# Own issue tables for the first and the last graph of a two-layer graph network on one Trainium2 core

## The chip, the cores and the metric

The kernel runs on one core of one Trainium2 chip. A core has five engines that each work through their own queue in order: TensorE (PE, matrix products; PEld is its loading of weights), VectorE (DVE), ScalarE (ACT), GpSimd (POOL) and SyncE (SP), which here issues all the DMA transfers. Times are device microseconds for one execution. The median of three runs of the kernel before is 1805.68 us (1802.11 to 1806.99); the execution that the profile shows took 1803.61 us, of which 1801.8 us are its span from the first to the last instruction.

## What is computed

There are 16 graphs of 1024 nodes with 256 features, and an adjacency matrix of 1024 x 1024 integers for each. The matrix is symmetric, holds zeros and ones, and has ones on the diagonal. Two layers follow each other; each ends in a residual sum and a normalization of rows.

```python
def _L0_gnn_ref(hidden, adj, a0, a1, a2, a3, bias):
    e_of = lambda a: _leaky(jnp.einsum('bid,bjd->bij', h * a[:, 0], h))
    alpha = jnp.where(adj == 1, e0, neg_inf)      # kinds 2, 3, 4 likewise
    alpha = jax.nn.sigmoid(alpha)
    return jnp.einsum('bij,bjd->bid', alpha, h) + bias

def _L1_gnn_ref(X, A, W, a_src, a_dst):
    Wh = (X @ W).reshape(B, N, H, F)              # 4 heads of 64
    e = leaky_relu(e_src[:, :, None, :] + e_dst[:, None, :, :], 0.2)
    alpha = softmax(where(A > 0, e, -1e9), axis=2)
    Hout = elu(einsum('bijh,bjhf->bihf', alpha, Wh))

x = _layernorm(x + _L0_gnn_ref(x, adj, ...))
x = _layernorm(x + _L1_gnn_ref(x, adj, ...))
```

## The kernel before, in words

The nodes of a graph are cut into eight blocks of 128. A graph's work is cut into stages, each a Python generator whose every step issues a few instructions. The table `TIMES` gives a due time in us for each step of each stage, relative to the graph's own start; graph b's steps are moved by 112 x b (`PERIOD`). `issue` (L861) sorts all steps of all 16 graphs by due time and runs them in that order. So the table fixes only the order in which instructions stand in each engine's queue, never a moment: an instruction runs as soon as it is at the head of its queue and its inputs are there. Due times of neighbouring graphs interleave, so that graph b+1's first layer is made while graph b is in its second.

The first layer of a graph, in the order of the data:

- `xload` (L231) fetches the nodes xb in one transfer of 1 MB; `aload` (L236) fetches the adjacency in eight row blocks of 512 KB into two buffers (a32).
- `cast` (L244, ACT) makes a block bf16 (a16, one buffer) and adds it up; `turn` (L253) transposes it by a DMA from the SP queue (aT, one buffer); `mask` (L259, ACT) squares it into the byte mask mT and adds that up.
- `xt` (L271, PE) transposes the nodes, `xtc` (L281, ACT) copies them out of PSUM, and `xta` (L291, ACT) multiplies them by the factors a0.
- `score` (L306, PE) makes the upper triangle of scores in twelve pieces; `leak` (L319, ACT), `leaky` (L327, DVE) and `sigmoid` (L333, ACT) turn each into a gate; `upper` (L363, DVE) masks a row of it, and `below` (L344, PE) with `lower` (L352, DVE) fills the lower triangle from the transposed upper one.
- `agg` (L370, PE) sums the nodes by the gates, 16 products for each pair of row blocks; `residual`, `moments`, `gathered`, `spread`, `shift` and `norm` (L388 to L439) are the residual and the normalization.

The second layer: `yt`, `ytc`, `project` and `wh` (L442 to L479) make the heads. `top_dve` (L506) ends with nd, the negated target terms. `exps` (L545) makes exponential factors es. For each of four heads and two slopes, `product` (L556, DVE) multiplies the 64 columns of a head by its factors (prod), `high` (L571, ACT) rounds the product and `low` (L577, DVE) takes what is left; both go into gm. `sload` (L585) fetches the source terms of a head, spread over all partitions (sbc); prod and sbc share four buffers. `pos` (L595, DVE) makes a 0/1 matrix (six buffers), `acc` (L605, PE) multiplies gm by it, `acc_low` (L620, ACT) and `acc_sum` (L629, DVE) collect it into u. `all_edges` (allm) and `total` do the same for the whole mask. `weigh` (L688, DVE) multiplies a part of u by rho, `divide` (L699, DVE) adds the parts and multiplies by the reciprocal of the softmax sum; `elu` (L729, ACT), `join` (L717, DVE), a second normalization and `leave` end the graph. After the last graph a small check (L1032 to L1050) decides whether a general path has to run; with these inputs it doesn't.

All PSUM tiles of one bank (nodes, scores, gates, sums) come from one pool of four buffers, `ps_t`.

Of the kernel before, what the change touches and what calls it, by code (L numbers as in the profile page):

```python
# [10 lines left out]
BF16 = mybir.dt.bfloat16  # L11
# [3 lines left out]
AF = mybir.ActivationFunctionType  # L15
ALU = mybir.AluOpType
# [11 lines left out]
P = 128  # L28
# [8 lines left out]
def load_constants(nc, const, work, x, a_list, bias, w, a_src, a_dst):  # L37
    k = Consts()
    B, N, D = x.shape
    H, F = a_src.shape  # L40
    k.B, k.N, k.D, k.H, k.F = B, N, D, H, F
    k.NB, k.DC, k.NH, k.WA = N // P, D // P, N // HALF, D + H
    k.WD = k.WA + H
    k.F1 = F + 2
    k.ident = const.tile([P, P], F32, name="ident")
    make_identity(nc, k.ident)
    k.mhalf = const.tile([P, 1], F32, name="mhalf")
    nc.gpsimd.memset(k.mhalf, -0.5)

    k.a_sb = const.tile([P, k.DC, NK], F32, name="a_sb")  # L50
    for i, a in enumerate(a_list):
        nc.sync.dma_start(out=k.a_sb[:, :, i : i + 1], in_=a.rearrange("(c p) o -> p c o", p=P))
    bias_bc = work.tile([P, D], F32, tag="bias_bc", name="bias_bc")
    nc.sync.dma_start(out=bias_bc, in_=bias.partition_broadcast(P))


    k.w_aug = const.tile([P, k.DC, k.WD], F32, name="w_aug")
    nc.sync.dma_start(out=k.w_aug[:, :, 0:D], in_=w.rearrange("(c p) f -> p c f", p=P))
    for a, which in ((a_src, 0), (a_dst, 1)):
        a_bc = work.tile([P, D], F32, tag="a_bc", name=f"a_bc{which}")  # L60
        nc.sync.dma_start(out=a_bc, in_=a.rearrange("h f -> (h f)").partition_broadcast(P))
        for c in range(k.DC):
            prod = work.tile([P, D], F32, tag="prod", name=f"prod{which}_{c}")
            nc.vector.tensor_tensor(prod, k.w_aug[:, c, 0:D], a_bc, ALU.mult)
            dst = k.w_aug[:, c, D + which * H : D + which * H + H]
            nc.vector.tensor_reduce(dst, prod.rearrange("p (h f) -> p h f", h=H), AX.X, ALU.add)

    k.ones_r = const.tile([P, P], F32R, name="ones_r")
    ones = work.tile([P, P], F32, tag="ones", name="ones")
    nc.gpsimd.memset(ones, 1.0)  # L70
    nc.scalar.copy(k.ones_r, ones)
    k.ones = k.ones_r.bitcast(F32)
    b_hi = work.tile([P, D], F32R, tag="b_hi", name="b_hi")
    nc.scalar.copy(b_hi, bias_bc)
    b_lo = work.tile([P, D], F32, tag="b_lo", name="b_lo")
    nc.vector.tensor_tensor(b_lo, bias_bc, b_hi.bitcast(F32), ALU.subtract)
    nc.vector.tensor_scalar(b_lo, b_lo, k.ident[:, 1:2], None, ALU.mult)
    k.bias_r = const.tile([P, D], F32R, name="bias_r")
    nc.vector.scalar_tensor_tensor(
        k.bias_r, b_hi.bitcast(F32), k.ident[:, 0:1], b_lo, ALU.mult, ALU.add  # L80
    )
    return k
# [127 lines left out]
def stages(nc, k, pl, b, xg, adjg, outg, gm, sums, span, zinv):  # L210


    H, F, D, N, NB, DC, NH = k.H, k.F, k.D, k.N, k.NB, k.DC, k.NH
    F1, WD = k.F1, k.WD
    NQ = NB // NH
    HEADS = [(half, h) for half in range(NH) for h in range(H)]

    TOTALS = [*range(NQ, NB), *range(NQ)]
    t = {}

    def bank(name):
# [30 lines left out]

    def turn():  # L253
        for ib in range(NB):
            t["aT", ib] = pl.adjp.tile([P, NB, P], BF16, tag="aT", name="aT", bufs=1)
            nc.sync.dma_start_transpose(out=t["aT", ib], in_=t["a16", ib])
            yield

    def mask():  # L259
# [21 lines left out]
    def xtc():  # L281
        t["xT"] = pl.big.tile([P, DC, N], F32, tag="xT", name="xT")
        for c in range(DC):
            for half in range(NH):
                nc.scalar.copy(
                    t["xT"][:, c, half * HALF : (half + 1) * HALF],
                    t["xt", c, half].rearrange("p q n -> p (q n)"),
                )
                yield

    def xta():  # L291
        for jb in range(NB):
            xTa = t["xTa", jb] = pl.work.tile([P, DC, P], F32, tag="xTa", name="xTa", bufs=2)
            for c in range(DC):
                nc.scalar.activation(  # L295
                    xTa[:, c, :], t["xT"][:, c, jb * P : (jb + 1) * P], AF.Copy,
                    scale=k.a_sb[:, c, 0:1],
                )
            yield


# [254 lines left out]
    def product():  # L556
        for h, s in FACTORS:
            prod = t["prod", h, s] = pl.work.tile(
                [P, NB, F], F32, tag="sbc", name="prod", bufs=4
            )  # L560
            nc.vector.tensor_tensor(  # L561
                prod, t["wh"][:, :, h * F : (h + 1) * F],
                t["es"][:, s, :, h : h + 1].to_broadcast([P, NB, F]), ALU.mult,
            )
            yield

    def factor(h, s):
# [117 lines left out]

    PAIRS = [(half, pair) for half in range(NH) for pair in range(NQ // 2)]

    def weigh():  # L688
        for half, pair in PAIRS:
            ib = half * NQ + 2 * pair  # L690
            u2 = parts(half, pair)[:, :, :, 1, :]
            if half:
                nc.vector.tensor_tensor(u2, t["ts", pair], u2, ALU.subtract)
                yield
            rho = t["rho"][:, ib : ib + 2].unsqueeze(3)
            nc.vector.tensor_tensor(u2, u2, rho.to_broadcast([P, 2, H, F1]), ALU.mult)
            yield

    def divide():  # L699
        t["rz"] = small("rzs", NB, H)  # L700
        for half, pair in PAIRS:
            ib = half * NQ + 2 * pair
            u = parts(half, pair)
            u1 = u[:, :, :, 0, :]
            nc.vector.tensor_tensor(u1, u1, u[:, :, :, 1, :], ALU.add)
            yield
            rz = t["rz"][:, ib : ib + 2]
            nc.vector.tensor_scalar(rz, u[:, :, :, 0, F], Z_MIN, None, ALU.max)
            yield
            nc.vector.reciprocal(rz, rz)  # L710
            yield
            o = u[:, :, :, 0, 0:F]
            nc.vector.tensor_tensor(o, o, rz.unsqueeze(3).to_broadcast([P, 2, H, F]), ALU.mult)
            yield


# [18 lines left out]
    def leave():  # L735
# [10 lines left out]
        xload=xload(), aload=aload(), cast=cast(), turn=turn(), mask=mask(),  # L746
        xt=xt(), xtc=xtc(), xta=xta(), score=score(), leak=leak(), leaky=leaky(),
        sigmoid=sigmoid(), below=below(), lower=lower(), upper=upper(), agg=agg(),
        residual=residual(), moments0=moments("0"), gathered0=gathered("0"),
        spread0=spread("0"), shift0=shift("0"), norm0=norm("0"),  # L750
        yt=yt(), ytc=ytc(), project=project(), wh=wh(), sources=sources(), rows=rows(), keep_rows=keep_rows(),
        top_dve=top_dve(), top_pe=top_pe(), exps=exps(),
        product=product(), high=high(), low=low(),
        sload=sload(), pos=pos(), acc=acc(), acc_low=acc_low(), acc_sum=acc_sum(),
        all_edges=all_edges(), total=total(), total_kept=total_kept(), total_less=total_less(),
        weigh=weigh(), divide=divide(), elu=elu(), join=join(),
        moments1=moments("1"), gathered1=gathered("1"),
        spread1=spread("1"), shift1=shift("1"), norm1=norm("1"), leave=leave(),
    )

# [93 lines left out]
    "norm1": [242.99, 243.17, 243.83, 247.18, 275.70, 276.83, 276.86, 278.99],  # L856
    "leave": [252.45, 280.64],
}


def issue(graphs):  # L861

    steps = []
    for b, stages in enumerate(graphs):
        for name, times in TIMES.items():
            steps += [(b * PERIOD + at, stages[name]) for at in times]
    for _, stage in sorted(steps, key=lambda step: step[0]):
        next(stage)
# [121 lines left out]
def gnn_resnorm_kernel(  # L990
# [64 lines left out]
    with tc.If(general > 0):  # L1055
        with ExitStack() as slow:
            pl = Pools(slow, tc, "g")
            k.w_dst_rep = pl.big.tile([P, k.DC, H, P], F32, tag="w_dst_rep", name="w_dst_rep")
            replicate(nc, k, k.w_dst_rep, D + H)
            k.ident16 = pl.big.tile([P, P], BF16, tag="ident16", name="ident16")  # L1060
            make_identity(nc, k.ident16)
            k.bias_bc = pl.big.tile([P, D], F32, tag="bias_bc", name="bias_bc")
            nc.sync.dma_start(out=k.bias_bc, in_=bias.partition_broadcast(P))
            with tc.For_i(0, k.B) as b:
                xg = x[bass.ds(b, 1)].rearrange("o n d -> (o n) d")
                adjg = adj[bass.ds(b, 1)].rearrange("o n m -> (o n) m")
                outg = out[bass.ds(b, 1)].rearrange("o n d -> (o n) d")
                xb, a16, y = load_graph(nc, k, pl, xg, adjg)
                alphaT = gate_any_kind(nc, k, pl, xb, a16)
                finish_graph(nc, k, pl, xb, a16, y, alphaT, outg)  # L1070
# [32 lines left out]
```

## Time and profile before

| what | us |
|---|---|
| median of three runs | 1805.68 |
| profiled execution | 1803.61 |
| its span | 1801.8 |
| PE busy | 1721.5 (96%) |
| VectorE busy | 1626.5 (90%) |
| ScalarE busy | 1181.7 (66%) |
| GpSimd busy | 111.4 (6%) |
| first product of `score` | 35.55 |
| first product of `agg` | 61.88 |
| median from issue to landing: adjacency block | 4.9 |
| the same: DMA transpose | 3.1 |
| the same: sbc | 4.5 |

In a line of the profile, L248 is the line of the kernel, out<-in are the tiles, 128x1024 is partitions x elements, and an arrow in brackets names what ended the idle time before the instruction. A group's line gives the number of instructions, their busy time, the mean ns of one, and the idle time before them. The mean of one holds also the time in which the next one already begins, so instructions that follow each other start closer than that.

### The profile page before, as it was taken

What the parts mean: (1) busy time and instruction counts of PE and PEld (TensorE: products, weight loads), DVE (VectorE), ACT (ScalarE), POOL (GpSimd) and SP (SyncE); (2) the same over time, 40 slices, a digit from 0 to 9 for tenths busy, and PEclk for the clock granted to TensorE, in tenths of its full rate; (3) what the DMA queues carried; (4) which work ended last, traced back from release to release, by engine and by line L of the source; (5) the groups of instructions that cost most, each with busy time, mean ns of one, the idle gap of its engine ahead of it and who ended that gap; (6) DMA issues with size and microseconds to landing.
All of it is one profiled execution on the core that took longest, in us unless ns stands there. A gap on an engine that the chain in (4) does not pass through costs nothing.

```text
span 1801.8 us, 29518 instructions
## 1 busy us (share of the span) xinstructions
PE 1721.5 (96%) x10643; PEld 1515.6 (84%) x10643; DVE 1626.5 (90%) x3577; ACT 1181.7 (66%) x2671; POOL 111.4 (6%) x136
## 2 busy tenths in 40 slices
PE   2999999999999999999999999999999999999983
PEld 1769899897988989799898989989898998979873
DVE  1467999999999999999999999999999999999997
ACT  4583775958568495766849476694957759484442
POOL 0000001000010100001010000100000010000100
PEclk8999999999999999999999999999999999999997
DMA  5523352433335243343433344243333424321111
GB/s 155 140 74 85 82 142 65 112 107 79 109 89 139 73 106 96 86 120 88 118 94 99 90 89 129 73 128 100 80 91 105 130 65 122 108 66 42 24 48 43
DMA packets 257689, 170.69 MB, mean 95 GB/s; under 512 B 141696, under 2 KB 241152, under 8 KB 257536
## 3 DMA queue, kind: packets, MB, share of 16 engines
q1 hardware_dynamic: 257536, 168.73, 35.3%
q8 instruction: 86, 1.41, 0.3%
q14 instruction: 67, 0.55, 0.1%
HBM read 118.10 MB, written 17.04 MB: 75 GB/s over the span
## 4 chain that ended last, share of the span: by engine, by line
PE 90%; DVE 3%; issue 3%; ACT 2%; DMA 1%; POOL 0%; SPq 0%; ACTq 0%; POOLq 0%; DVEq 0%
PE acc L611 26%; PE agg L377 25%; PE tot L654 14%; PE e L310 13%; PE pw L466 6%; PE pg L349 3%; PE pt L447 1%; PE pt L276 1%; DVE pos L599 1%; PE agg L373 1%; DMA a<-in_adj_dram 1%; DMA aT<-a 1%; DVE gm L581 0%; ACT a L248 0%; DVE prod L561 0%
## 5 line engine op out<-in xcount | busy, mean ns | idle before, releaser
L599 DVE SCALAR_TENSOR_TENSOR pos<-sbc,nd,mT 128x512 fp32r<-128x512 f32 x1024 | 730.3, 741 | 41.3 <-PE acc L611 40.5
L611 PE MATMUL acc<-gm,pos 128*128 128x264 f32 x4096 | 626.9, 298 | 17.2 <-DVE u L634 11.9
L611 PEld LDWEIGHTS acc<-gm,pos 128*128 128x128 f32 x4096 | 545.1, 190 | 41.7 <-issue 13.0
L377 PE MATMUL agg<-xb,gate 128*128 128x256 f32 x2048 | 474.5, 380 | 1.8 <-DVE gate L366 1.8
L377 PEld LDWEIGHTS agg<-xb,gate 128*128 128x128 f32 x2048 | 375.5, 190 | 46.3 <-DVE gate L366 2.0
L654 PE MATMUL tot<-gm,allm 128*128 128x264 f32 x2048 | 322.5, 299 | 2.7 <-ACT allm L646 1.7
L626 ACT COPY low<-acc 128x264 f32<-128x264 f32 x256 | 89.7, 376 | 314.8 <-PE acc L611 310.0
L654 PEld LDWEIGHTS tot<-gm,allm 128*128 128x128 f32 x2048 | 281.5, 189 | 7.6 <-ACT allm L646 2.2
L310 PE MATMUL e<-xT,xTa 128*128 128x512 f32 (+3 forms) x768 | 272.7, 493 | 10.5 <-ACT xTa L295 10.0
L310 PEld LDWEIGHTS e<-xT,xTa 128*128 128x128 f32 x768 | 133.5, 192 | 103.9 <-issue 47.3
L646 ACT CAST allm<-mT 128x512 fp32r<-128x512 uint8 x256 | 156.8, 619 | 27.5 <-PE tot L654 27.5
L434 ACT ACTIVATE y<-y,shift,rstd 128x256 f32<-128x256 f32 x256 | 137.5, 592 | 47.4 <-DVE shift L427 47.4
L263 ACT ACTIVATE mT<-aT 128x1024 uint8<-128x1024 bf16 x128 | 135.4, 1058 | 27.6 <-DMA aT<-a 27.6
L248 ACT ACTIVATE a<-a 128x1024 bf16<-128x1024 int32 x128 | 135.3, 1057 | 10.5 <-DMA aT<-a 6.4
L330 DVE TENSOR_TENSOR gate<-e,gate 128x512 f32<-128x512 f32 x192 | 104.1, 549 | 39.2 <-ACT gate L322 39.1
L417 POOL TENSOR_SCALAR std<-mv 128x4 f32<-128x4 f32 x64 | 30.1, 470 | 1676.0 <-DVE mv L400 1523.3
L466 PE MATMUL pw<-w_aug,yT 128*128 128x264 f32 x512 | 124.2, 386 | 0.2 <-ACT yT L456 0.2
L634 DVE TENSOR_TENSOR u<-acc,low 128x264 f32<-128x264 f32 x256 | 104.1, 417 | 6.5 <-ACT low L626 6.5
L466 PEld LDWEIGHTS pw<-w_aug,yT 128*128 128x128 f32 x512 | 92.7, 190 | 13.2 <-ACT yT L456 0.7
L394 DVE BATCH_NORM_STATS2 st<-y 128x6 f32<-128x256 f32 x256 | 101.9, 414 | 0.6
L322 ACT ACTIVATE gate<-e 128x512 f32<-128x512 f32 x192 | 93.1, 485 | 11.8 <-PE e L310 11.8
L366 DVE TENSOR_TENSOR gate<-gate,mT 128x1024 f32<-128x1024 f32 (+7 forms) x128 | 94.6, 750 | 4.7 <-PE pg L349 2.9
(92 smaller groups left out, 1771.8 us busy)
## 6 DMA issues: line engine op xcount, KB each, us to landing
a<-in_adj_dram SPq DMA_DIRECT2D x128, 512.0 KB, 4.9
sbc<-sdram SPq DMA_DIRECT2D x128, 256.0 KB, 4.5
xb<-in_x_dram SPq DMA_DIRECT2D x16, 1024.0 KB, 5.8
out_dram<-y SPq DMA_DIRECT2D x32, 512.0 KB, 3.5
aT<-a SPq DMA_TRANSPOSE x128, 3.1
sdram<-srow SPq DMA_DIRECT2D x32, 8.0 KB, 1.4
w_aug<-in_L_gnn_W_dram SPq DMA_DIRECT2D x1, 256.0 KB, 4.6
bias_bc<-in_L_gnn_bias_dram SPq DMA_DIRECT2D x1, 128.0 KB, 4.2
```

Source lines behind the costliest of these rows:

```text
L248: nc.scalar.activation(t["a16", ib], t["a32", ib], AF.Copy, accum_out=sums[:, 0, at : at + 1])
L263: nc.scalar.activation(t["mT"][:, :, ib * P : (ib + 1) * P], t["aT", ib], AF.Square, accum_out=sums[:, 1, at : at + 1],)
L310: nc.tensor.matmul(e[:, 0:n], lhsT=t["xTa", jb][:, c, :], rhs=t["xT"][:, c, at : at + n], start=(c == 0), stop=(c == DC - 1),)
L330: nc.vector.tensor_tensor(ge, t["e", jb, at][:, 0:n], ge, ALU.max)
L377: nc.tensor.matmul(agg[:, 0:D], lhsT=t["gate"][:, jb, ib * P : (ib + 1) * P], rhs=t["xb"][:, jb, :], start=False, stop=(jb == NB - 1),)
L434: nc.scalar.activation(y, y, AF.Identity, bias=t["shift" + which, half][:, q : q + 1], scale=t["rstd" + which, half][:, q : q + 1],)
L466: nc.tensor.matmul(pw[:, 0:WD], lhsT=t["yT"][:, c, jb * P : (jb + 1) * P], rhs=k.w_aug[:, c, :], start=(c == 0), stop=(c == DC - 1),)
L599: nc.vector.scalar_tensor_tensor(p_, t["sbc", half, h], t["nd"][:, jb, h : h + 1], t["mT"][:, jb, half * HALF : (half + 1) * HALF], ALU.is ...
L611: nc.tensor.matmul(t["acc", half, h, q // 2][:, q % 2, 0 : 4 * F1], lhsT=t["pos", half, h, jb][:, q * P : (q + 1) * P], rhs=gm[:, h, jb].r ...
L634: nc.vector.tensor_tensor(t["u", half, pair][:, :, h, :], t["acc", half, h, pair][:, :, 0 : 2 * F1], t["low", half, h, pair], ALU.add,)
L646: nc.scalar.copy(m_, t["mT"][:, j0 : j0 + 4, ib * P : (ib + 1) * P])
L654: nc.tensor.matmul(tot[:, 0 : H * F1], lhsT=t["allm", ib, jb // 4 * 4][:, jb % 4, :], rhs=gm[:, :, jb, l, 1, :], start=(jb == 0 and l == 0 ...
```

## The change

There are two more tables of the same form, `FIRST` for graph 0 and `LAST` for graph 15; graphs 1 to 14 keep `TIMES`. In `FIRST` all steps of graph 0's first layer up to the statistics lie ahead of every step of graph 1, where in `TIMES` graph 1's loads, casts, transposes and masks are mixed in. In `LAST` most of graph 15's second layer lies after the end of graph 14.

In graph 0, moreover, `turn` transposes on PE into PSUM (with a bf16 identity that is now made at the start), eight 128x128 pieces a block, and `xtc` and `xta` run on DVE. In graph 15, the multiplies of `product`, `weigh` and `divide` run on ACT, in pieces that have one factor per partition: eight for a product, eight for a pair of row blocks.

```diff
+    k.ident16 = const.tile([P, P], BF16, name="ident16")
+    make_identity(nc, k.ident16)
...
+    first, last = b == 0, b == k.B - 1
...
     def turn():
         for ib in range(NB):
-            t["aT", ib] = pl.adjp.tile([P, NB, P], BF16, tag="aT", name="aT", bufs=1)
-            nc.sync.dma_start_transpose(out=t["aT", ib], in_=t["a16", ib])
+            if first:
+                t["aT", ib] = pl.ps_t.tile([P, NB, P], BF16, tag="pt", name="pa")
+                for jb in range(NB):
+                    nc.tensor.transpose(
+                        t["aT", ib][:, jb, :], t["a16", ib][:, jb * P : (jb + 1) * P], k.ident16
+                    )
+            else:
+                t["aT", ib] = pl.adjp.tile([P, NB, P], BF16, tag="aT", name="aT", bufs=1)
+                nc.sync.dma_start_transpose(out=t["aT", ib], in_=t["a16", ib])
             yield
...
-                nc.scalar.copy(
+                copy = nc.vector.tensor_copy if first else nc.scalar.copy
+                copy(
                     t["xT"][:, c, half * HALF : (half + 1) * HALF],
...
-                nc.scalar.activation(
-                    xTa[:, c, :], t["xT"][:, c, jb * P : (jb + 1) * P], AF.Copy,
-                    scale=k.a_sb[:, c, 0:1],
-                )
+                part, a = t["xT"][:, c, jb * P : (jb + 1) * P], k.a_sb[:, c, 0:1]
+                if first:
+                    nc.vector.tensor_scalar(xTa[:, c, :], part, a, None, ALU.mult)
+                else:
+                    nc.scalar.activation(xTa[:, c, :], part, AF.Copy, scale=a)
...
-            nc.vector.tensor_tensor(
-                prod, t["wh"][:, :, h * F : (h + 1) * F],
-                t["es"][:, s, :, h : h + 1].to_broadcast([P, NB, F]), ALU.mult,
-            )
+            if last:
+                for jb in range(NB):
+                    nc.scalar.activation(
+                        prod[:, jb, :], t["wh"][:, jb, h * F : (h + 1) * F], AF.Copy,
+                        scale=t["es"][:, s, jb, h : h + 1],
+                    )
+            else:
+                nc.vector.tensor_tensor(
+                    prod, t["wh"][:, :, h * F : (h + 1) * F],
+                    t["es"][:, s, :, h : h + 1].to_broadcast([P, NB, F]), ALU.mult,
+                )
...
+    def times(val, by):
+        if last:
+            for q in range(2):
+                for h in range(H):
+                    nc.scalar.activation(
+                        val[:, q, h, :], val[:, q, h, :], AF.Copy, scale=by[:, q, h : h + 1]
+                    )
+        else:
+            by = by.unsqueeze(3).to_broadcast(list(val.shape))
+            nc.vector.tensor_tensor(val, val, by, ALU.mult)
...
-            rho = t["rho"][:, ib : ib + 2].unsqueeze(3)
-            nc.vector.tensor_tensor(u2, u2, rho.to_broadcast([P, 2, H, F1]), ALU.mult)
+            times(u2, t["rho"][:, ib : ib + 2])
...
-            o = u[:, :, :, 0, 0:F]
-            nc.vector.tensor_tensor(o, o, rz.unsqueeze(3).to_broadcast([P, 2, H, F]), ALU.mult)
+            times(u[:, :, :, 0, 0:F], rz)
...
+FIRST = {
+    "xload": [-2609.24],
+    "aload": [-1820.92, -1748.01, -1728.96, -1693.97, -1643.68, -1598.12, -1550.35, -1517.97],
...
+LAST = {
+    "xload": [-104.45],
...
+    "product": [93.84, 98.53, 107.41, 108.99, 117.90, 120.96, 121.69, 130.00],
...
     for b, stages in enumerate(graphs):
-        for name, times in TIMES.items():
+        table = FIRST if b == 0 else LAST if b == len(graphs) - 1 else TIMES
+        for name, times in table.items():
             steps += [(b * PERIOD + at, stages[name]) for at in times]
```

## The prediction

> **What bounds the kernel now.** I read the totals, then busy time cut by stage, then the two ends in order of time, and last the durations kept apart by shape.
>
> ```profile
> PE 1721.5 (96%) x10643; PEld 1515.6 (84%) x10643; DVE 1626.5 (90%) x3577; ACT 1181.7 (66%) x2671; POOL 111.4 (6%) x136
> ```
>
> 96% TensorE (PE) is a mean over different stages. By stretch (from:to, length, then busy us and instructions of PE, PEld, VectorE = DVE, ScalarE = ACT and POOL; granted clock, DMA share, GB/s):
>
> ```profile
> 0.00:20.00 20.00, 0.00 (x0) 0.00 (x0) 4.75 (x13) 5.33 (x10) 0.86 (x8) 1.00 0.57 142
> 20.00:40.00 20.00, 8.09 (x22) 5.14 (x23) 0.00 (x0) 10.38 (x22) 0.00 (x0) 0.77 0.68 192
> 40.00:62.00 22.00, 18.11 (x68) 10.10 (x66) 10.56 (x19) 21.43 (x46) 0.00 (x0) 0.97 0.43 108
> 62.00:93.00 31.00, 31.00 (x145) 27.09 (x146) 12.06 (x33) 9.33 (x20) 1.27 (x2) 0.95 0.50 136
> 93.00:121.00 28.00, 25.01 (x110) 16.71 (x109) 15.76 (x40) 26.20 (x64) 1.27 (x2) 0.94 0.25 66
> 121.00:300.00 179.00, 179.00 (x1143) 161.16 (x1142) 162.04 (x344) 113.63 (x255) 8.26 (x10) 1.00 0.37 99
> 300.00:1680.00 1380.00, 1379.92 (x8637) 1221.70 (x8636) 1312.52 (x2885) 952.24 (x2157) 91.47 (x104) 1.00 0.37 97
> 1680.00:1701.00 21.00, 20.16 (x121) 18.02 (x120) 19.09 (x52) 9.38 (x25) 2.02 (x2) 1.00 0.00 1
> 1701.00:1722.00 21.00, 14.46 (x78) 12.66 (x77) 19.72 (x44) 9.20 (x27) 2.04 (x2) 0.76 0.24 64
> 1722.00:1760.00 38.00, 31.16 (x240) 29.88 (x239) 38.00 (x78) 15.88 (x35) 1.65 (x2) 1.00 0.12 31
> 1760.00:1782.00 22.00, 14.24 (x94) 13.10 (x94) 21.18 (x47) 3.25 (x8) 1.26 (x2) 0.92 0.12 32
> 1782.00:1802.00 20.00, 0.37 (x1) 0.08 (x1) 10.87 (x32) 5.41 (x10) 1.26 (x2) 0.58 0.17 57
> ```
>
> From 121 to 1680 PE has no gap: there only less PE work helps, and the change takes none away. What can move is the head, where PE lacks 20 + 11.9 + 3.9 + 3.0 = 38.8 us before 121, and the tail, where from 1701 to 1782 DVE is busy 78.9 of 81 us. A head that is shorter moves everything behind it one for one.
>
> The head is a relay for each of the eight blocks of graph 0's adjacency: load, cast (L248), DMA transpose (L256), mask (L263). In ScalarE's timeline:
>
> ```profile
> 14.58 1.06 ACT L248 ACTIVATE a<-a 128x1024 bf16<-128x1024 int32 x1 [3.34 <-DMA aT<-a]
> ...
> 31.57 1.06 ACT L263 ACTIVATE mT<-aT 128x1024 uint8<-128x1024 bf16 x1 [3.12 <-DMA aT<-a]
> ```
>
> Each block waits some 3.1 us for its transpose, and the pace is about 6 us a block. Row 0 of the gate needs all eight masks (L366 takes all of mT's row), so the aggregation starts only at
>
> ```profile
> 61.88 5.21 PE L377 MATMUL agg<-xb,gate 128*128 128x256 f32 x16 [1.80 <-DVE gate L366]
> ```
>
> and ends at 92.8, 30.9 us of dense PE. In the tail these DVE groups are what the change moves, and two ACT groups are the nearest to what it puts in their place:
>
> ```profile
> L561 DVE TENSOR_TENSOR prod<-wh,es 128x512 f32<-128x512 f32 x128 | 86.3, 684 | 2.1 <-ACT es L547 1.3
> ...
> L696 DVE TENSOR_TENSOR u<-u,rho 128x528 f32<-128x528 f32 x64 | 44.0, 688 | 0.0
> L713 DVE TENSOR_TENSOR u<-u,rzs 128x512 f32<-128x512 f32 x64 | 43.5, 679 | 0.0
> ```
> ```profile
> L434 ACT ACTIVATE y<-y,shift,rstd 128x256 f32<-128x256 f32 x256 | 137.5, 592 | 47.4 <-DVE shift L427 47.4
> ...
> L295 ACT ACTIVATE xTa<-xT,a_sb 128x128 f32<-128x128 f32 x256 | 88.9, 401 | 0.0
> ```
>
> **The head, part by part.** *SP queue.* Eight transposes leave it (1.24 us of issue each, 3.1 to land), and xb is issued sixth from the front, ahead of the adjacency. Between 7 and 10 us the DMA moved the first two adjacency blocks at 360 to 397 GB/s; xb's 1 MB, at the 311 to 319 it later had, now takes that place: xb at 10.4 instead of 23.8, block 0 at 11.8 instead of 10.1. The a_dst row (L61) is still issued at about 10.1 and lands near 13; queued behind it are block 1 (about 14) and, behind two buffers, the rest, each some 3.7 us after the cast that frees its buffer. *DVE* takes four node copies (ACT 0.59 each; 0.55 to 0.6 on DVE by L330's 549 ns) and 16 factor multiplies (0.2 each from L77's 0.34 for twice the width), 5.7 us in a stretch where it has nothing. But L64's product with a_dst stands between the first two copies, so copies 2 to 4 wait until 13, and PE's first score behind them until 16.4. *ACT* is rid of 7.8 us (4 x 0.59, 16 x 0.34). *POOL* builds the bf16 identity first (0.20 + 0.29 us), which delays ones, which ACT casts behind b_hi at 7.4: nothing needs it before the aggregation.
>
> *Transposes on PE.* 64 of 128x128. Nearest: L349 warm, four in 0.66 us, 0.13 each; L276 cold, 16 in 3.65, 0.23. So 1.0 to 1.8 us a block instead of 3.1 + 1.24. They stand in PE's in-order queue between the scores, so a late cast holds up the scores and leak (L322) and leaky (L330) after them; a16 has one buffer, so each cast waits for the transpose before it. The Trainium skill, "TensorE: Matmul & The Clock Gate", section "Part 1: The HAM clock gate", speaks against this: PE runs at half clock until about 3.4 us of sustained work. The trace: scores took 0.85 us from 35.5 and 0.43 only after 41.5, six us. PE's work before the aggregation is 20 us warm, 36 cold. By the rule taken alone (sparse work stays cold) PE is busy from 10.4 to 46.4 or later; by the row, PE is nearly without a gap from the first score at 16.4 and warm by 22.5. I take the row.
>
> Walking the built order with these durations, the masks end at 17.5, 21, 26.5, 27.7, 33.5, 36.5, 38.3 and 41.8; the multiply of row 0 (1.1) lets the aggregation start at 43. The bounds: ACT alone, from block 0 at 11.8, needs 24 us up to the last mask (16 casts and masks at 1.04, eight leaks 4.1, a table load 1.28, two sigmoids 2.0) and row 0 its 1.1, so not before 37; at 5 us a block, 52. The aggregation then takes 30.9 + 2.1 (17 transposes of gate against 6, and two small scores, that now fall into it) = 33: end at 76 instead of 92.8. Graph 1's casts, masks and transposes, which ran between graph 0's, now come behind its sigmoids, at about 53; three blocks at 5.5 us put graph 0's first normalization, queued behind them on ACT, at 69 to 72, before PE asks for it at 76. That is the cover, 4 us; without it what is late is yt and projection. From there to 121 the relay is that of before. **Head: -16.5 us** (-24 to -8).
>
> **The tail.** DVE loses 8 products at 0.605 (start to start, two in 1.29), 4 weights at 0.62, 4 divisions at 0.60: 9.7 us. ACT gets 64 + 32 + 32 activations of 128x64 or 66 with a scale from memory. The trace has none. From L295 (401 ns; two in 0.68, so 0.28 start to start) and 64 columns fewer, about 0.23. The skill's "ScalarE: Activation LUTs", section "What ACT_TABLE_LOAD costs", states 186 + 93 for the pointer + 0.833 a column, less 93 of overlap: 0.24. Its section "Rules for kernel authors" says the opposite of this change: multiplies belong on VectorE. Indeed a factor costs 1.9 us on ACT against 0.605; by the rule the tail would lose. By the stage it gains, since DVE is full there and ACT has 53 of 81 us free. I take 0.235.
>
> What comes late: the first two factors are ready 7 us after nd (L532) instead of 3, behind 16 multiplies and two copies of low for graph 14 in ACT's queue; all eight after 24. DVE has other work ordered ahead of them (graph 14's sums, eight pos, its weights), which covers it but for about 1.5 us; sbc, in the same four buffers, may cost 1 (4.5 us to land). At the end, 32 activations lie between the last acc_sum and the last norm; two pairs overlap, and by my walk low to last norm is 15.8 us, 15.1 before. Two more table loads (1.28 each), while graph 15's gate is made, lie under PE. **Tail: -9.7 + 1.5 + 1 + 0.7 = -6.5 us** (-9.7 to +1).
>
> Graphs 1 to 14 keep their table and their order among themselves. **Sum:** the profiled execution took 1803.6 us, 1801.8 of it span; minus 23.0 is 1780.6. The median of the three runs lies 2.1 above the profiled one, so 1782.7: **1783 us**.
>
> **Rivals.** *The head's gain is half gone (15%).* PE stays cold, or a block waits for PE behind a score, and the aggregation starts at 50 to 52: head -8, tail -5, 1793. For: clock 0.77 between 20 and 40. Against: that stretch had PE 60% idle. *The tail gives nothing (12%).* Late factors idle DVE: 1789. Against: DVE's ordered work. *ACT is the head's only limit (10%).* Start at 37, and the tail in full: 1805.7 - 23 - 9 = 1774. *Slower (3%).* One mechanism: the price p of a scaled activation. All eight factors are ready after 8.7 + 64p, with 24.9 us of DVE work ahead, and 24 lie in series at the end: loss 88p - 21.8 against the forecast, which eats 23 us from p = 0.51 on. L434 reaches 0.50, but with 256 columns and two pointers; at 0.60 it is 1783 + 31 = 1814. *No difference (5%)*: the waits only move, graph 1's masks holding up the norm, say; 1803.
>
> **How the numbers follow.** The forecast holds 55%, within 1776 to 1790. Faster by over 0.3% (5.4 us, about what a measurement can tell from no change): 55 + 15 + 12 + 10 = 92%; within: 5%; slower: 3%. The range 1770 to 1798 holds the first four.
>
> **What would show it.** Right: first L377 near 43, its last near 76, the three DMA waits for aT gone before it; PE full from about 105; between nd and the last acc_sum about 73.5 us instead of 80.4; scaled activations of 128x64 near 0.33 each. Wrong: agg after 50; PE at half clock through the head; DVE waiting for gm; an end chain over 18 us.

## Result and the profile after

| what | before | after |
|---|---|---|
| median, us | 1805.06 (1802.11 to 1806.99, 4 runs) | 1781.75 (1780.34 to 1782.10, 4 runs) |
| ratio, 95% interval | | 0.9871 (0.9854 to 0.9888) |
| profiled execution, and its span | 1803.61, 1801.8 | 1781.79, 1780.0 |
| first and last product of `agg`, graph 0 | 61.88, 92.8 | 40.75, 72.6 |
| nd of graph 0, nd of graph 15 | 106.0, 1701.1 | 85.5, 1680.4 |
| nd of graph 15 to the last sum of a head | 80.6 | 77.9 |
| nd of graph 15 to the end of the span | 100.7 | 99.6 |

23.3 us less; 23.0 was forecast. The totals, then busy time by stage (from:to, length, busy us and instructions of PE, PEld, DVE, ACT, POOL; granted clock, DMA share, GB/s), both of the changed kernel:

```profile
PE 1718.5 (97%) x10707; PEld 1517.1 (85%) x10707; DVE 1624.8 (91%) x3581; ACT 1208.9 (68%) x2781; POOL 112.1 (6%) x138
```
```profile
0.00:20.00 20.00, 7.27 (x39) 5.49 (x40) 7.56 (x21) 6.66 (x12) 1.27 (x10) 1.00 0.64 190
20.00:41.00 21.00, 17.05 (x95) 9.96 (x94) 9.37 (x22) 19.83 (x39) 0.00 (x0) 1.00 0.43 151
41.00:73.00 32.00, 32.00 (x165) 28.24 (x165) 16.28 (x44) 13.48 (x27) 1.27 (x2) 1.00 0.42 114
73.00:101.00 28.00, 25.72 (x124) 18.04 (x123) 16.77 (x40) 26.48 (x64) 1.27 (x2) 1.00 0.35 87
101.00:300.00 199.00, 198.33 (x1263) 178.20 (x1263) 180.50 (x393) 126.34 (x293) 12.91 (x14) 1.00 0.36 94
300.00:1659.00 1359.00, 1358.42 (x8497) 1201.79 (x8496) 1292.98 (x2831) 940.64 (x2118) 87.83 (x101) 1.00 0.37 97
1659.00:1680.00 21.00, 20.21 (x123) 18.10 (x122) 19.01 (x51) 11.16 (x28) 1.68 (x2) 1.00 0.01 2
1680.00:1701.00 21.00, 9.90 (x56) 9.51 (x56) 17.66 (x42) 19.33 (x78) 1.27 (x2) 0.76 0.09 26
1701.00:1739.00 38.00, 35.46 (x268) 35.21 (x269) 36.58 (x76) 23.00 (x58) 2.03 (x2) 0.91 0.24 70
1739.00:1758.40 19.40, 13.73 (x88) 12.47 (x87) 17.29 (x35) 9.11 (x33) 0.00 (x0) 0.91 0.00 1
1758.40:1780.00 21.60, 0.37 (x1) 0.08 (x1) 10.81 (x36) 12.85 (x42) 2.53 (x4) 0.52 0.16 53
```

The rows are cut 21 us earlier than those of before. PE works from 12 us on, and the dense aggregation (row 41 to 73) starts at 41 instead of 62. The clock of 1.00 in the first row does not mean full clock from the start: this column also reads 1.00 where the trace has no record of the clock, and the first record here, of full clock, stands at 14.85 us. What came before it is seen in the durations, here of the same transposes of nodes in graph 0 and in graph 1:

```profile
11.94 3.35 PE L287 MATMUL pt<-ident,xb 128*128 128x128 f32 x16 [11.94 <-DMA xb<-in_x_dram]
...
82.44 0.60 PE L287 MATMUL pt<-ident,xb 128*128 128x128 f32 x4
```

In the first line most start 0.21 us apart, in the second 0.11; within the first line the step comes at 14.85. So PE began at half clock and had full clock 2.9 us after its first product.

From 101 to 1659 PE lacks 1.2 of 1558 us: the middle hands the head's gain on, and from nd of graph 0 to nd of graph 15 it is 1595.1 us before and 1594.9 after. The second row shows the new limit of the head: ACT is busy 19.83 of 21 us. In its timeline and PE's the waits of 3.1 us for a DMA transpose are gone:

```profile
13.06 1.06 ACT L252 ACTIVATE a<-a 128x1024 bf16<-128x1024 int32 x1 [5.89 <-DMA a<-in_adj_dram]
...
38.29 1.06 ACT L274 ACTIVATE mT<-pa 128x1024 uint8<-128x1024 bf16 x1
```
```profile
16.53 1.96 PE L323 MATMUL e<-xT,xTa 128*128 128x512 f32 x4 [0.79 <-DVE xTa L309]
18.32 0.61 PE L262 MATMUL pa<-ident,a 128*128 128x128 bf16 x8
...
40.75 1.56 PE L390 MATMUL agg<-xb,gate 128*128 128x256 f32 x6
```

A block's transpose is 0.61 us on PE, ScalarE goes from casts to masks to `leak` with few pauses, and the last mask ends at 39.35. In the tail, the groups of instructions show the new multiplies:

```profile
L576 ACT ACTIVATE prod<-wh,es 128x64 f32<-128x64 f32 x64 | 15.9, 338 | 0.0
L713 ACT ACTIVATE u<-u,rho 128x66 f32<-128x66 f32 x32 | 8.2, 338 | 2.1 <-DVE u L701 1.1 <-DVE u L725 1.0
L713 ACT ACTIVATE u<-u,rzs 128x64 f32<-128x64 f32 x32 | 8.1, 336 | 2.1 <-DVE rzs L741 2.1
```

Start to start that is 15.9 / 64 = 0.25 us each. What VectorE waits for between nd and the last sum of a head (engine, line, releaser: us in total, times, longest), after and then before:

```profile
DVE u L654 <- ACT low L646: 4.3, 4, 1.9
DVE gm L601 <- ACT gm L594: 1.4, 3, 0.9
DVE pos L619 <- PE acc L631: 0.8, 2, 0.6
```
```profile
DVE u L634 <- ACT low L626: 2.1, 2, 1.2
```

By these two traces alone the gain would be 20.7 in the head and only 1.1 behind nd. That was the reading (theory 2 below) with which the experiments began, and it fell.

### The profile page after: what moved, and what is told of

Read it like the earlier page. It is cut to its first block, busy times and chain, and to the rows that moved or that the text cites. A ratio compares the mean times of both kernels' runs of the same rounds, so it can differ in the third digit from the quotient of the medians.

```text
span 1780.0 us, 29755 instructions
## 1 busy us (share of the span) xinstructions
PE 1718.5 (97%) x10707; PEld 1517.1 (85%) x10707; DVE 1624.8 (91%) x3581; ACT 1208.9 (68%) x2781; POOL 112.1 (6%) x138
## 4 chain that ended last, share of the span: by engine, by line
PE 86%; issue 8%; ACT 2%; DVE 1%; POOL 1%; DMA 0%; POOLq 0%; ACTq 0%
PE acc L631 25%; PE agg L390 23%; PE tot L674 13%; PE e L323 13%; PE pw L479 6%; PE pg L362 3%; PE pt L287 1%; PE pt L460 1%; PE agg L386 1%; POOL rstd L432 1%; DVE pos L619 0%; ACT gm L594 0%; ACT a L252 0%; PE pbc L553 0%; ACT L349 0%
## 5 line engine op out<-in xcount | busy, mean ns | idle before, releaser
L631 PEld LDWEIGHTS acc<-gm,pos 128*128 128x128 f32 x4096 | 547.7, 191 | 41.5 <-issue 15.9
L323 PEld LDWEIGHTS e<-xT,xTa 128*128 128x128 f32 x768 | 131.5, 190 | 92.8 <-issue 45.6
L274 ACT ACTIVATE mT<-aT 128x1024 uint8<-128x1024 bf16 x120 | 127.1, 1059 | 16.0 <-DMA aT<-a 15.9
L654 DVE TENSOR_TENSOR u<-acc,low 128x264 f32<-128x264 f32 x256 | 104.6, 420 | 12.8 <-ACT low L646 12.6
L335 ACT ACTIVATE gate<-e 128x512 f32<-128x512 f32 x192 | 93.6, 488 | 18.4 <-PE e L323 18.3
```

The lines of the kernel that those rows point to most:

```text
L274: nc.scalar.activation(t["mT"][:, :, ib * P : (ib + 1) * P], t["aT", ib], AF.Square, accum_out=sums[:, 1, at : at + 1],)
L323: nc.tensor.matmul(e[:, 0:n], lhsT=t["xTa", jb][:, c, :], rhs=t["xT"][:, c, at : at + n], start=(c == 0), stop=(c == DC - 1),)
L631: nc.tensor.matmul(t["acc", half, h, q // 2][:, q % 2, 0 : 4 * F1], lhsT=t["pos", half, h, jb][:, q * P : (q + 1) * P], rhs=gm[:, h, jb].r ...
L654: nc.vector.tensor_tensor(t["u", half, pair][:, :, h, :], t["acc", half, h, pair][:, :, 0 : 2 * F1], t["low", half, h, pair], ALU.add,)
```

## Experiments

Medians of 4 runs unless said otherwise. The kernel before had 1805.39 us beside `head_alone`, `tail_alone`, `first_dma` and `first_turn_only`, 1807.14 beside the four parts of the tail, and 1804.72 beside `first_copies_act` and the two splits. The changed kernel was not run again beside them, so a difference of 1 or 2 us between kernels of different groups is not shown by the medians. "Undone" is against the changed kernel, 1781.75.

### The two halves alone

`head_alone`: graph 15 as before.

```diff
-        table = FIRST if b == 0 else LAST if b == len(graphs) - 1 else TIMES
+        table = FIRST if b == 0 else TIMES
-            if last:        # product, and the same in times
+            if False:
```

> Graph 0 as changed (table FIRST, transposes on TensorE, copies and factors on VectorE); graph 15 as in the kernel before. Theory 1, the forecast's split (head -16.5, tail -6.5): 1805 - 16.5 = 1788.5 us. Theory 2, read off the trace of the changed kernel (the nd of graph 15 came 20.7 us earlier, and only 1.1 to 1.4 us are gained behind it): 1805 - 20.7 = 1784.4 us, with nd of graph 15 near 1680.4, and the last sum of a head 80.5 us behind it as in the kernel before. Rival: without the new tail something of the head's gain is lost on the way through graphs 14 and 15: over 1790.

`tail_alone`: graph 0 as before (the same edits for `first`).

> Graph 15 as changed (table LAST, multiplies on ScalarE); graph 0 as in the kernel before. Theory 1: 1805 - 6.5 = 1798.5 us. Theory 2: 1805 - 1.3 = 1803.7 us, which cannot be told from no change by the median, but by the trace: nd to the end of the span 99.6 us instead of 100.7, VectorE waiting for gm and for low by turns. Aggregation of graph 0 at 61.9 in both.

Head alone: 1787.01 us (1784.29 to 1787.48), ratio 0.9891 (0.9873 to 0.9909), 18.4 us. Tail alone: 1801.51 us (7 runs, 1799.66 to 1802.88), ratio 0.9975 (0.9963 to 0.9988), 3.9 us. The product of the ratios, 0.9866, is within the interval of the whole change: the halves add up, the head to more than the forecast's 16.5 and the tail to less than its 6.5. Neither theory had both right. In `head_alone` nd of graph 15 came at 1680.0, as theory 2 said, but from there to the end it took not 100.7 us but 105.0, in the same order of instructions as before. So the tail of before isn't one number. The next run was made for this.

### A second trace of the kernel before

`before_again`: nothing is edited.

> The kernel before, unchanged, for a second trace. Its runs spread over 7.6 us (1801.2 to 1808.8), those of the changed kernel over 1.8. Theory C: the spread is TensorE's clock in the tail; in the first trace of before a pause of 3 us near 1740 left the clock at 1.00, in the trace of the head alone the same pause in the same order of instructions was followed by half clock, and its tail from nd to the end took 105.0 us instead of 100.7. Then a trace with a time of 1806 or more shows half clock between 1735 and 1782 and a tail of some 104 to 106 us, and nd again near 1701. Theory D: the spread comes from the head: nd moves, the tail stays at 100.7.

1804.86 us, span 1803.1; nd of graph 15 at 1698.5, and 104.6 us from there to the end. Theory C holds for the tail: the same pause, at full clock in the first trace, and at half in the second. Stretches of 4 us, first trace:

```profile
1738.00:1742.00 4.00, 1.01 (x9) 0.80 (x7) 4.00 (x7) 1.69 (x4) 0.00 (x0) 1.00 0.22 66
1742.00:1746.00 4.00, 3.52 (x27) 3.48 (x28) 4.00 (x9) 0.00 (x0) 0.00 (x0) 1.00 0.00 0
```

and the second, cut 2.6 us earlier as nd was:

```profile
1735.40:1739.40 4.00, 1.42 (x12) 1.20 (x10) 4.00 (x8) 1.70 (x4) 0.00 (x0) 0.98 0.22 66
1739.40:1743.40 4.00, 3.32 (x15) 3.32 (x16) 3.81 (x8) 0.00 (x0) 0.00 (x0) 0.50 0.00 0
```

At clock 0.50, PE did 15 products in 3.32 us of work instead of 27 in 3.52. VectorE then waits for it (second trace, waits of VectorE from nd to the last sum, 5.3 us against 2.1 above):

```profile
DVE u L634 <- ACT low L626: 3.7, 2, 2.2
DVE pos L599 <- PE acc L611: 1.6, 2, 1.0
```

VectorE's work was the same, 78.5 and 78.9 us. Theory D holds for a smaller part: nd of graph 15 also came 2.6 us earlier, and 2.1 of these were there at graph 0's nd (103.9 instead of 106.0). In the head the clock differed too. The first 20 scores, in the first trace and in the second:

```profile
35.55 11.13 PE L310 MATMUL e<-xT,xTa 128*128 128x512 f32 x20 [8.12 <-ACT xTa L295]
```
```profile
35.67 10.26 PE L310 MATMUL e<-xT,xTa 128*128 128x512 f32 x20 [7.68 <-ACT xTa L295]
```

At full clock the same 20 take 8.70 us (graph 1 of the changed kernel, shown with `first_copies_act`). In both traces the first of them start 0.85 us apart, half clock, and the later ones 0.43; full clock came at 41.04 in the first trace and at 39.41 in the second. When the aggregation began, the clock of the first trace fell once more and that of the second did not:

```profile
61.50:65.00 3.50, 3.12 (x8) 2.54 (x9) 3.50 (x6) 0.68 (x3) 0.00 (x0) 0.51 0.52 98
```
```profile
61.50:65.00 3.50, 3.50 (x18) 3.09 (x18) 3.13 (x5) 0.45 (x2) 0.00 (x0) 1.00 0.67 137
```

So the first trace, which the forecast was made from, had an unlucky head and a lucky tail. Against the second the change brings 18.1 us up to nd and 104.6 - 99.6 = 5.0 behind it, near what the two halves gave. That the clock makes up all of the spread of before (1801.23 to 1808.77 in 26 runs) is likely but shown in two traces only.

### The parts of the head

`first_dma`: the transposes go by DMA again.

```diff
-            if first:       # in turn
+            if False:
```

> The changed kernel with one part undone: the eight transposes of graph 0 go by DMA from the SP queue again; table FIRST, copies on VectorE and the tail stay. Theory T, the transposes on TensorE carry the head: a block costs cast 1.06 + transpose 3.1 + mask 1.06 = 5.2 us in series from block 0 at about 13, so eight end near 55, aggregation near 56, and the time is 1781.8 + 56 - 40.8 = 1797 us. Theory O, the order of the table carries it (graph 0's blocks no longer behind other work, other work on ScalarE fills the 3.1 us): aggregation at 44 to 46 and 1785 to 1787 us.

1808.28 us (20 runs, 1806.29 to 1809.67), 26.5 above the changed kernel and slower than before: 1.0014 (1.0007 to 1.0021). Theory T named the right part, but its 56 was too early; the aggregation began at 64.01. ScalarE's waits from 10 to 64 show why:

```profile
ACT mT L274 <- DMA aT<-a: 11.8, 4, 3.2
ACT a L252 <- DMA a<-in_adj_dram: 11.4, 3, 5.5
ACT a L252 <- issue: 3.9, 1, 3.9
ACT a L252 <- DMA aT<-a: 3.3, 2, 2.4
```

15.1 us are the transposes themselves. Another 11.4 are late blocks of the adjacency. They are issued from the same queue as the transposes, and in SP's own waits from 0 to 64 the transposes (L267) hold it up at six waits for the one before and two for the cast, among others:

```profile
SPq L267 <- DMA aT<-a: 10.0, 6, 3.1
...
SPq L267 <- ACT a L252: 6.3, 2, 3.7
SPq L243 <- ACT a L252: 5.8, 2, 4.6
```

L243 is the load of a block, behind its buffer. PE was also at a clock of only 0.64 from 40 to 64; what that cost was not separated. So `FIRST` is an order for transposes that take 0.61 us; with those of 3.1 it is worse than `TIMES` (`tail_alone`, 1801.51).

`first_turn_only`: graph 0 in the order of `TIMES`.

```diff
-        table = FIRST if b == 0 else LAST if b == len(graphs) - 1 else TIMES
+        table = LAST if b == len(graphs) - 1 else TIMES
```

> The changed kernel with another part undone: graph 0 is ordered by TIMES again, with its transposes on TensorE, its copies and factors on VectorE; the tail stays. Theory T: the masks are no longer the last thing that row 0 waits for; the nodes, which land at 23.8 in that order, are, and the aggregation starts at 46 to 50: 1787 to 1791 us. Theory O: the order holds everything up as before, the aggregation starts at 56 or later: 1797 us or more.

1789.30 us (1788.87 to 1789.42), 7.5 undone; the aggregation starts at

```profile
50.73 1.56 PE L390 MATMUL agg<-xb,gate 128*128 128x256 f32 x6 [0.94 <-DVE gate L379]
```

0.7 later than Theory T said, with a time inside its range. The new order brings 7.5 us, but only on top of the new engines: with the transposes by DMA it lost. The engines bring 12.2 in the old order (against 1801.51 for `tail_alone`); there the transposes and the copies were not run apart.

`first_copies_act`: graph 0's node copies and factors on ScalarE.

```diff
-                copy = nc.vector.tensor_copy if first else nc.scalar.copy
+                copy = nc.scalar.copy
-                if first:       # in xta
+                if False:
```

> The changed kernel with the third part of its head undone: graph 0's four node copies and sixteen factor multiplies are on ScalarE again; table FIRST, transposes on TensorE and the tail stay. Theory A, ScalarE now sets the pace of the head (busy 19.0 of 20 us between 20 and 40): it gets 4 x 0.59 + 16 x 0.28 = 6.8 us back, of which some 2 us fit into its pauses before 20, so the aggregation starts 4 to 7 us later and the time is 1786 to 1789 us. Theory B, the blocks' arrival and TensorE set it: the aggregation moves by under 2 us, 1782 to 1784 us.

1787.37 us (1785.80 to 1787.73), 5.6 undone; the aggregation starts at 44.38, 3.6 later. This is Theory A, a little under its 4 to 7: with 6.8 us more, ScalarE has no pause left between 20 and 40.

```profile
20.00:40.00 20.00, 15.06 (x82) 8.24 (x80) 5.04 (x8) 19.92 (x42) 0.00 (x0) 1.00 0.48 161
```

The median moved more than the start of the aggregation. The profiled execution took 1785.80, 4.0 more than that of the changed kernel: 3.6 up to nd of graph 0, 1.2 from there to nd of graph 15 (1596.1 us), and 0.8 less behind it. The 1.2 are PE's clock at the first scores of graph 1, which stand behind the same pause of 1.42 us in both; first the changed kernel, then this one with the row over it:

```profile
87.14 8.70 PE L323 MATMUL e<-xT,xTa 128*128 128x512 f32 x20 [1.42 <-ACT xTa L311]
```
```profile
90.77 10.06 PE L323 MATMUL e<-xT,xTa 128*128 128x512 f32 x20 [1.42 <-ACT xTa L311]
90.00:94.00 4.00, 3.23 (x4) 1.50 (x5) 3.75 (x7) 3.48 (x13) 0.00 (x0) 0.59 1.00 238
```

The traces of `last_weights`, `last_products` and `split_end` below have the same dip (10.12 us) and took 1595.9 to 1596.1 from nd to nd. `head_alone`, `last_order`, `last_engines`, `split_both` and `first_dma` took 8.70 there, as the changed kernel did, and 1594.5 to 1595.0. Why the other three executions of `first_copies_act` took 1.3 to 1.9 us more than the profiled one stays open.

### The parts of the tail

Four kernels keep the new head. `last_order` has table `LAST` with all multiplies on VectorE, `last_engines` has `TIMES` with all of them on ScalarE, `last_weights` puts only the products back on VectorE, `last_products` only weights and divisions.

```diff
-        table = FIRST if b == 0 else LAST if b == len(graphs) - 1 else TIMES
+        table = FIRST if b == 0 else TIMES      # last_engines
-            if last:        # in product: last_order, last_weights
+            if False:
-        if last:            # in times: last_order, last_products
+        if False:
```

> The changed kernel with the multiplies of graph 15 back on VectorE; its table LAST and the new head stay. Theory E, the engines carry the tail's gain: VectorE has its 9.7 us back, less the 3.1 us that it waits for gm in the changed kernel, so about 1781.8 + 5 = 1787 us, as with the head alone (1787.0). Theory R, the order LAST carries it: 1781 to 1783 us. The first two factors are ready 3 us after nd again in both.

> The changed kernel with graph 15 ordered by TIMES; its multiplies stay on ScalarE and the new head stays. Theory E: about 1782 to 1784 us. Theory R: the factors come late and VectorE's queue has in its old order nothing else ahead of them, so that it waits for gm much longer than 3.1 us: 1787 us or more.

> The changed kernel with only the eight products of graph 15 back on VectorE; weights and divisions stay on ScalarE. If what the late factors cost (1.9 us for the first, 1.2 us in waits for gm, and TensorE at half clock after its pause of 5 us) is as large as what the products cost VectorE (8 x 0.605 = 4.8 us), nothing changes: 1781 to 1783 us. If the late factors cost only what the forecast gave them (1.5 us, and 1 for sbc): 1784 to 1785 us. If the pause of TensorE costs more than the waits show: under 1780 us.

> The changed kernel with only the weights and divisions of graph 15 back on VectorE (8 instructions at 0.61, 4.9 us, two pairs of them before the last sum of a head, two after it); the products stay on ScalarE. The forecast gives ScalarE's end chain +0.7 us, so undoing it takes 0.7 off the end and puts 2.4 us on VectorE ahead of the last sum: 1783 to 1784 us. By the trace of the changed kernel (16.9 us from low to the last normalization instead of 15.1) 1.8 comes off the end: 1782 to 1783 us. If VectorE isn't the limit ahead of the last sum: 1780 us.

The three columns in the middle are of the profiled execution, from nd of graph 15 to the last sum of a head: its length, VectorE's busy time, and the rest, in which it waits. The last is from there to the end of the span.

| kernel | median, us | length | VectorE busy | VectorE waits | to the end |
|---|---|---|---|---|---|
| after | 1781.75 | 77.9 | 71.1 | 6.9 | 21.7 |
| head_alone | 1787.01 | 84.1 | 78.9 | 5.2 | 20.9 |
| last_order | 1787.87 | 82.7 | 77.8 | 4.9 | 22.4 |
| last_engines | 1796.00 | 87.8 | 72.5 | 15.3 | 25.7 |
| last_weights | 1785.36 | 80.9 | 75.4 | 5.5 | 21.6 |
| last_products | 1786.13 | 80.5 | 73.5 | 7.0 | 22.6 |
| split_end | 1781.58 | 77.6 | 71.1 | 6.5 | 21.2 |
| split_both | 1782.09 | 78.3 | 71.8 | 6.5 | 21.0 |

With the order `LAST`, Theory E holds: `last_order` came within 1 us of its 1787. The length is VectorE's work plus its waits. The products, put back, add 4.3 us of work and take 1.4 of the waits away; weights and divisions add 2.4. So the late factors don't balance the products, which was one expectation: `last_weights` lost 3.6 us. `last_products` lost 4.4, more than all three of its expectations: the part behind the last sum, which was to become shorter, became 0.9 longer, and 1.1 us were lost ahead of nd, in the dip of the clock shown above. The order alone gives nothing (0.9 slower than the head alone). For `last_engines`, Theory R was right: the multiplies on ScalarE alone, in the old order, cost 9.0 us more than the head alone. VectorE's and PE's waits in `last_engines`, in the same stretch, tell why:

```profile
DVE gm L601 <- ACT gm L594: 7.9, 6, 4.1
DVE u L654 <- ACT low L646: 6.1, 4, 2.2
```
```profile
PE acc L631 <- ACT prod L576: 7.0, 1, 7.0
PE tot L674 <- ACT gm L594: 4.5, 1, 4.5
```

In `TIMES` the factors are the first thing behind nd, so VectorE stands 4.1 us before the first and 7.9 before all; in `LAST` it does other work ahead of them and waits 1.4. By the medians the order is worth 9.0 + 5.3 = 14.3 us once the multiplies are on ScalarE. The two traces differ by 13.9 behind nd: 8.4 are VectorE's waits before the last sum (15.3 against 6.9), 1.4 its work, and 4.0 lie behind the last sum, where VectorE waits 7.4 us for ScalarE's multiplies and `elu` in `last_engines` and 1.4 in the changed kernel. So the order covers late results at both ends of the stretch.

### Splitting what ScalarE does in series

```diff
+            if half:        # in times, for the last two pairs: split_end, split_both
+                nc.vector.tensor_tensor(val[:, 0], val[:, 0],
+                    by[:, 0].unsqueeze(2).to_broadcast(list(val[:, 0].shape)), ALU.mult)
-            for q in range(2):
+            for q in range(half, 2):
...
+                cut = NB // 2 if h < 1 else 0       # in product: split_both
```

> The changed kernel, with the multiplies of the last two pairs of graph 15 (the last two weights and divisions) split: VectorE multiplies the first block of each pair in one instruction, ScalarE the second in four. If the two pairs' 32 pieces (7.9 us on ScalarE, in series after the last sum) set the end: 1.5 to 2.5 us off, 1779 to 1780 us. If VectorE's own work sets it there (10.9 of 21.7 us): 1781 to 1783 us, as now.

> The kernel with the split end, and the first two factors of graph 15 split as well: VectorE multiplies four of the eight blocks (+0.3 us each), ScalarE the other four (-1 us each). If the 1.4 us that VectorE waits for gm and TensorE's pause of 5 us after it cost time: another 0.5 to 1.5 us off, 1778 to 1779.5 us. If VectorE's load alone counts: 0.6 us more than with the split end.

1781.58 us (1781.32 to 1783.11) and 1782.09 (1781.32 to 1782.82): no difference from the changed kernel that can be measured. The faster times of their first expectations (1778 to 1780) did not come; both fit the other one, that VectorE's own work counts. After the last sum ScalarE lost 3.5 us of work, VectorE got 1.1 more, and the end came 0.4 us sooner:

```profile
1758.40:1780.00 21.60, 0.37 (x1) 0.08 (x1) 10.81 (x36) 12.85 (x42) 2.53 (x4) 0.52 0.16 53
```
```profile
1760.12:1781.30 21.18, 0.37 (x1) 0.08 (x1) 11.92 (x40) 9.34 (x26) 2.53 (x4) 0.51 0.17 53
```

(the changed kernel from 1758.4, then `split_end`). Even that 0.4 is not certain to be the split's: the four other kernels with the unsplit end of `LAST` on ScalarE (`tail_alone` and the three parts of the head) took 21.2 to 21.5 us there. So ScalarE's series alone doesn't set the end; which chain does was not isolated. No kernel tried beats the changed one by a difference that can be measured.

## Why the prediction was right

The time was met (1783 forecast, 1781.75 measured), and each half came from the mechanism that was forecast. The terms are less exact than their sum: head -16.5 against -18.4, tail -6.5 against -3.9 alone and -5.3 on top of the head. That the two misses nearly cancel is luck. Step by step:

- **"A head that is shorter moves everything behind it one for one."** Shown: 1594.5 to 1596.1 us from nd to nd, whatever the head, in every trace compared.
- **Block 0 at 11.8, xb at 10.4.** Too early; the cast came at 13.06 and xb at 11.94. The first score at 16.4 was right (16.53).
- **"1.0 to 1.8 us a block"** for a transpose on PE. This term was mis-sized: 0.61, or 0.08 a piece, below both rows (0.13 and 0.23) it was scaled from. Those are f32 pieces, these are bf16; start to start at full clock they are 0.11 and 0.06 apart. Over eight blocks that is 3 to 9.5 us of PE, not all on the path. In `first_turn_only` the blocks turned early, while PE was still at half clock, took 1.03.
- **PE at half clock until 22.5.** This was mis-sized too: full clock came at 14.85 and stayed through the head. The row "0.85 us from 35.5 and 0.43 only after 41.5", which the forecast took, was one execution's; the second trace of the same kernel had full clock 3.7 us after its first score (39.41), not after six. And the count starts at the transposes (11.94), not at the first score. The Trainium skill's "TensorE: Matmul & The Clock Gate", section "Part 1: The HAM clock gate", says that half clock is the default and that about 3.4 us of sustained work end it; the 2.9 us here are nearer to that than to the row. It also says that the window runs freely, so that its phase differs from run to run. The heads and tails of before look like that, but no run here set the phase.
- **Masks until 41.8, aggregation at 43.** 39.35 and 40.75. From block 0 to the last mask ScalarE took 26.3 us and not the 30 of the walk, with 24 of work by the forecast's own sum. It was to wait 6 us and waited 3.0, all for PE. Both terms above go that way; no run tells them apart.
- **Aggregation 33 us, then cover of 4 us for the first normalization.** 31.9 (40.75 to 72.6), all at full clock; the 30.9 that the forecast began from had 3.4 us at half clock in it (61.5 to 65, above). Graph 1's first cast came at 52.28, graph 0's first normalization at 68.49, PE asked at 72.47: the cover was 4.0 us.
- **DVE loses 9.7 us.** Of these, 8 products, two weights and two divisions lie ahead of the last sum: 4.84 + 1.24 + 1.20 = 7.3 us at the forecast's prices. Measured 78.9 - 71.1 = 7.8 against the head alone.
- **Late factors +1.5, sbc +1, end +0.7.** VectorE waits 1.4 us for gm; no wait for sbc is in the list. From the end of the last low to that of the last normalization it took 16.3 us, and 14.4 with the head alone and before (not the forecast's 15.1): 1.9 more, not 0.7. Of this, 0.8 reached the end behind the last sum (21.7 against 20.9). The order does it, not the multiplies: `last_order`, with these on VectorE, took 17.0 and 22.4. The low copies of graph 14, behind two products in ScalarE's queue, cost next to nothing: VectorE waits 1.90 for the first, and 1.38 in `last_order`, where no products are ahead of it.
- **"About 73.5 us instead of 80.4"** failed as it stands (77.9). The step was to take one execution's tail as the kernel's. Against the other two tails with the old code, 84.1 and 84.5, the change is -6.2 and -6.6, near the -6.9 meant.
- **Price 0.235**, an estimate. 0.25 measured. "Rules for kernel authors" in the skill's "ScalarE: Activation LUTs" puts multiplies on VectorE; here a factor costs 15.9 / 8 = 2.0 us on ScalarE against 0.6 on VectorE, and the move still wins 5.3 us, by the runs, because VectorE was full, ScalarE wasn't, and the order covered the late results.

Of the rivals, "the head's gain is half gone" did not come, since PE had full clock from 14.85. "ACT is the head's only limit" was nearest in mechanism: the last mask ended at 39.35, the limit given for it was 36, and the later block 0 (1.3) is part of the difference; `first_copies_act` shows that work added to ScalarE delays the aggregation. "The tail gives nothing" looked true in the first comparison and was refuted by `head_alone`. "Slower" would have needed twice the price; but `last_engines` shows a loss by another mechanism, the cover of the late factors.

## What to carry to other kernels

Where the middle is bound by one engine without gaps, what is gained up to its first dense stretch arrives whole; look in such a head for the engine that takes over as the limit, and take its side work away as well. Moving a stage to an engine three times slower pays if the fast engine is full there and if the order puts enough other work ahead of the consumers; without the reordering the same move lost 9 us, and the reordering without the move nothing. Stretches full of short pauses of PE are not one number: take a second trace before a few us of them are laid to a change.

## What the runs showed of the hardware

PE began at half clock in each of the heads looked at. Full clock came 2.9 us after the first product in the changed kernel (14.85) and 3.6 in the first trace of before (23.78 to 27.39, half again from 30.8). In the second, PE's first work ended after 3.7 us without it, and it came 3.7 us into the next (35.67 to 39.41). Ahead of the first record the profile's clock column says 1.00, so there the durations decide.

The same pause in the same order of instructions was followed by full clock in one execution and by half in another. Ahead of graph 1's first scores it was 1.42 us: half clock in four traces, full in six. In the tail of the old code: full after 3.47 us in the first trace of before, half after 3.47 in `head_alone` and after 3.26 in the second trace of before, which made its tail 4 us longer. With the changed tail, the five traces that have it whole (the changed kernel, `tail_alone` and the three parts of the head) lie within 98.7 and 99.6 us from nd to the end. There PE pauses for 5.15 to 5.18 and for 6.02 us while the factors are made, and was at half clock behind both in each of the five. In these traces the longer pauses always lost the clock and the shorter ones only sometimes, which fits the narrow spread of the changed kernel (1.8 us in 4 runs). What decides for a shorter pause stays open.
